# Attention steps with the values of two key steps in one run, another order for the maxima's scores, two merging DMAs a unit, and last units summed without GpSimd

## The chip, the cores and the metric

One core of a Trainium2 chip runs the whole kernel. The metric is the device time of one execution in microseconds. The median of three runs of the kernel before is 1054.57 us (1052.63 to 1055.07).

## The reference

A transformer block: attention with LoRA projections, residual and layer norm, then a mixture of experts (8 experts, one chosen per token, capacity 256) with a shared expert, residual and layer norm. The change touches attention alone:

```python
q = _split(lora_linear(x, Wq, bq, Bq, Aq))      # x: (2, 1024, 512), 16 heads of 32
k = _split(lora_linear(x, Wk, bk, Bk, Ak))
v = _split(lora_linear(x, Wv, bv, Bv, Av))
scores = jnp.einsum('bhqd,bhkd->bhqk', q, k) * SCALE
attn = jax.nn.softmax(scores, axis=-1)
out = jnp.einsum('bhqk,bhkd->bhqd', attn, v)
out = out.transpose(0, 2, 1, 3).reshape(B, L, H * hd)
return lora_linear(out, Wo, bo, Bo, Ao)
```

All of it is in float32. The kernel splits operands in a high and a low part[...] and adds the products.

## The kernel before, in words

Attention is cut into 16 units (NU): two batches, four groups of four heads, two halves of the queries (512 each). A unit has eight steps, one for each 128 keys; there are 128 steps (NS), numbered t, with u = t // 8 and k = t % 8. Step t does, for each of its four heads (the quarters q of the step):

- `st_step` (L611): the transposed scores `st`, 128 keys by 512 queries, one matmul on PE (TensorE) into a PSUM tile of the pool `one` (three tiles; L620), then the exponential on ACT into `pt` (L629). A `pt` tile holds two heads, 128 x 1024. There are 14 of them, so seven steps' worth.
- after each head, what the list `between[q]` holds.

What is put there:

- `s1_step` (L182): the scores a second time, not transposed, 12 steps ahead (LEAD), into a PSUM tile of `s1p` (three tiles; L189); VectorE (DVE) takes the maximum of each row (L197). One a quarter, so four a step and 32 a unit. `finish_max` transposes a unit's maxima on PE (`mp`, also a tile of `one`), and two DMAs put them beside the queries, so that `st` comes out with the maximum taken off. It is called with a quarter of the following unit's first step, number MPP.
- `av_step(t - 1)` (L633): the values of the step before: for each head a matmul with 32 output columns, four heads side by side in the array, summed over the eight steps in a PSUM tile `av{u}` (two such tiles). In a trace each of these float32 matmuls is two records, so a step has eight.
- `adds(t - 1)` (L648): the sums of the exponentials over keys. The table `ADDS` says, for a step of a unit, what is added: "b" names the tile that collects, "p" adds a tile to it on POOL (GpSimd), "v" on DVE, each for both tiles of a step (the two letters stand for the two tiles), and "d" is a DMA from POOL's queue that adds one step's tile into the next step's tile (a merging DMA; L656).
- `finish(u - 1)` (L666): matmuls with a matrix of ones sum the collected tile over its 128 rows into `sm` (a tile of `one`); the steps in `DIRECT` (step 7) go into it directly. For units below RDIR (13), ACT copies `sm` out and it goes by DRAM into a layout of 128 x 16, so that the reciprocal is short; from RDIR on DVE takes the reciprocal of 128 x 512 at once (L682).
- `invert(u - 1)` (L693): that short reciprocal, a store, and four DMAs that broadcast it back (`rb`). It stands after step 5.
- `normalize` (L706) in three parts: DVE multiplies `av` with the reciprocals (L711), ACT, or DVE for units in NRM_DVE, copies the high part (L716, L714), DVE subtracts to get the low part (L718).
- residual loads and adds (`load_res`, `add_res`, an add on POOL), and from step 65 on the output projection of the first batch (`oproj`), whose matmuls are spread over the steps.

Each engine works in the order in which the program lists its instructions; these steps are in a manual schedule (L763), so the order is the one written. SP, the queue of most DMAs, is such an engine too. A waiting instruction holds what stands behind it on its engine.

After the last step come `av_step`, `adds` and `finish` of unit 15, then output projections of the second batch and the first work of the experts, in an order that TAIL lists. The projections `op10` and o1 to o3 need unit 14 alone, o4 and later ones unit 15.

Of the kernel before, what the change touches and what calls it, by code (L numbers as in the profile page):

```python
# [20 lines left out]
NU = 16  # L21
# [11 lines left out]
LEAD = 12  # L33
LATE, OP_ONE = (0,), 1
NS = NU * 8
# [14 lines left out]
}  # L50
MAN3 = {mybir.EngineType.PE}
MAN4 = MAN2 - MAN3
DIRECT = (7,)
NO_DIR = (NU - 2,)
FIN, FINQ = 4, 1
REC = 5
NRM = 0
K_AT = 6
XTB = 5


ADDS = {
    None: {0: "bb0", 2: "dd1", 3: "pp3", 4: "pp4", 5: "pp2", 6: "pp5", 7: "pp6"},
    NU - 3: {0: "bb0", 2: "dd1", 3: "pp3", 4: "pp4", 5: "pp2", 7: "dd6 pp5"},
    NU - 2: {1: "bb1 dd0", 3: "dd2", 5: "dd4", 6: "vv3", 7: "vv6 vv7 vv5"},
    NU - 1: {0: "bb0", 1: "vp1", 2: "vp2", 3: "vp3", 4: "vp4", 5: "vp5", 6: "vv6"},
}
OPROJ_AT = (65, 67, 69, 71, 73, 75, 77, 79)
RES_AT = tuple(8 * i + (2 if i % 2 else 6) for i in range(8)) + (70, 74, 86, 90, 100, 102, 106, 110)
RES_ADDS = tuple(t + 3 for t in RES_AT[:14]) + (119, 120)  # L70
RB = 2
# [1 line left out]
AHEAD = 5  # L73
W2_END = {2: (0, 1, 2), 3: (3, 4), 4: (5,)}
W2_AT = {2: (0, 1), 3: (2, 3), 4: (4,), 5: (5,)}
MPJ, MPP = 0, 2
RDIR = NU - 3
FINE, NRME = 3, {NU - 2: 6, NU - 1: 5}
OPROJ1 = 0
NRM_DVE = (NU - 3, NU - 2)  # L80
ROOT_LAG, NORM_LAG = 1, 4
# [17 lines left out]
def kernel(  # L99
# [5 lines left out]
    def f(ap):  # L105
        return ap.bitcast(F32)
# [98 lines left out]
    def finish_max(u):  # L205
        mp = one.tile([P, 512], F32, name=f"mp{u}", tag="one")
        pe.transpose(mp[0:16, 0:P], mts[u], ident)
        mh = mp_.tile([16, P], F32R, name=f"mh{u}", tag="mh", bufs=2)
        ml = mp_.tile([16, P], F32R, name=f"ml{u}", tag="ml", bufs=2)
        act.copy(mh, mp[0:16, 0:P])  # L210
        dve.tensor_tensor(ml, mp[0:16, 0:P], f(mh), ALU.subtract)
        for i, m_ in enumerate((mh, ml)):
            sp.dma_start(
                out=f(Qs[u % 3][96 + i : 97 + i, :, :]).rearrange(
                    "o h (q t) -> o (h q) t", t=P
                ),
                in_=f(m_),
            )
# [382 lines left out]
    with ph2, tc.manual_schedule(engines={mybir.EngineType.PE}):  # L601
# [57 lines left out]
                        eng.tensor_tensor(accs[u, pr], accs[u, pr], pts[i, pr], ALU.add)  # L659

        def direct(u):
            return () if u in NO_DIR else DIRECT

        fin = {}

# [95 lines left out]
        op10 = oproj(1, 0, 3)  # L761
        steps = ExitStack()
        steps.enter_context(tc.manual_schedule(engines=MAN2))  # L763
        for t in range(NS):
            u, k = t // 8, t % 8
            if k == 0:
# [12 lines left out]
            if t in RES_AT:  # L779
                load_res(RES_AT.index(t))  # L780
            between = [[], [], [], []]
            if t + LEAD < NS:
                for q in range(4):
                    between[q].append(lambda q=q: s1_step(t + LEAD, q))
            elif t + LEAD == NS:
                between[0].append(lambda: finish_max(NU - 1))
            if t:
                between[1].append(lambda: av_step(t - 1))
                between[1].append(lambda: adds(t - 1))
                if u and k == (FINE if u == NU - 1 else FIN):  # L790
                    between[1 if u == NU - 1 else FINQ].append(lambda: finish(u - 1))
            if u:
                if k == NRM and 1 < u < NU - 1:
                    for q in range(3):
                        between[q].append(lambda q=q: normalize(u - 2, (q,)))
                if k == NRME.get(u):
                    for q in range(3):
                        between[(0, 3, 3)[q]].append(lambda q=q: normalize(u - 1, (q,)))
            if t in RES_ADDS:
                between[3].append(lambda: add_res(RES_ADDS.index(t)))  # L800
            st_step(t, between)
            if k == REC and 1 <= u <= RDIR:
                invert(u - 1)
            if t in OPROJ_AT:
                op0 = oproj(0, OPROJ_AT.index(t), OPER)
            if OPROJ_AT[0] <= t:
# [5 lines left out]
            later[:] = [(n - 1, fn) for n, fn in later if n]  # L812
            if t - NS >= OPROJ1:
                next(op10, None)
        av_step(NS - 1)
        adds(NS - 1)
        finish(NU - 1)
# [458 lines left out]
```

## Time and profile before

| | |
|---|---|
| median of three runs | 1054.57 us |
| the profiled execution | 1057.79 us |
| its span (first to last instruction) | 1056.1 us |
| mean granted TensorE clock | 0.992 |
| attention steps, first `st` of step 0 to that of step 127 | 155.82 to 601.15 us |
| first output projection after them | 614.54 us |
| first matmul of the shared expert | 640.82 us |

The page lists each engine's busy time, then groups of instructions by line: out<-in with shapes and count, then busy time, mean ns of one, and the idle time of that engine just before them with what ended most of it. PEld is TensorE's weight load, which runs beside matmuls. In a timeline a row has the start and the length in us, engine, line and tiles; rows of one kind in a row are merged with their count, and square brackets tell idle time before it and who ended it. Matmuls are pipelined, so a matmul's row of 0.40 us can be followed by the next after 0.235. A start to start distance is the cost; idle PE between two rows does not show where rows overlap.

Busy time by stretch (us from the span's start, busy us):

| stretch | PE | DVE | ACT | POOL |
|---|---|---|---|---|
| 225 to 255 | 29.47 | 23.49 | 20.29 | 29.47 |
| 285 to 315 | 30.00 | 24.40 | 19.86 | 29.77 |
| 375 to 405 | 29.75 | 20.82 | 14.73 | 26.60 |
| 525 to 555 | 30.00 | 24.32 | 19.85 | 30.00 |
| 585 to 605 (20 us) | 19.35 | 19.86 | 14.65 | 14.85 |
| 605 to 640 (35 us) | 28.72 | 26.58 | 9.48 | 19.45 |

The granted clock is 1.00 in all of these but the last, where it is 0.90.

### The profile page before, as it was taken

To read this page: it belongs to the slowest core of one execution; us is meant where nothing else is said; L and a number is where in the kernel's file an instruction comes from. 1 tells how busy PE (TensorE), PEld (TensorE's weight loads), DVE (VectorE), ACT (ScalarE), POOL (GpSimd) and SP (SyncE) were. 2 spreads that over 40 slices of the span, in tenths; PEclk is the share of its full clock that TensorE was granted. 3 is DMA by queue.
4 is the path that set the end of the run, shared out by engine and by line. 5 is a ranking of instruction groups with operands and counts; after the bars stand their busy time and mean duration, and the time that the engine had idled before them with its cause. 6 is when DMAs were issued, how large, how long until landed. Compare 5 with 4: busy or idle time off the path is not lost. (4 is left out here: it accounts for less than half of the span.)

```text
span 1056.1 us, 16556 instructions
## 1 busy us (share of the span) xinstructions
PE 1030.1 (98%) x5994; PEld 742.5 (70%) x5994; DVE 696.0 (66%) x1191; ACT 527.1 (50%) x1023; POOL 585.9 (55%) x407
## 2 busy tenths in 40 slices
PE   8999999999999999999999889999999999999995
PEld 6888774444444456544444359899999999999994
DVE  7732788778888877778887974233522557777752
ACT  5422216666666655566666716222222447555552
POOL 4000006999999986979995655000050046766674
PEclk9999999999999999999999989999999999999998
DMA  9866863454646553535648123000073456777721
GB/s 294 278 225 212 253 194 91 91 135 104 137 93 148 119 127 81 126 85 123 146 115 184 21 60 111 21 21 20 21 244 107 130 175 232 254 249 245 259 84 60
DMA packets 85449, 149.83 MB, mean 142 GB/s; under 512 B 15428, under 2 KB 24132, under 8 KB 85368
## 3 DMA queue, kind: packets, MB, share of 16 engines
q1 hardware_dynamic: 76344, 117.31, 37.5%
q0 software_dynamic: 9024, 31.48, 12.4%
q8 instruction: 47, 0.77, 0.3%
q14 instruction: 34, 0.28, 0.1%
HBM read 95.83 MB, written 33.78 MB: 123 GB/s over the span
## 5 line engine op out<-in xcount | busy, mean ns | idle before, releaser
L197 DVE TENSOR_REDUCE mt<-s 128x1 f32<-128x512 f32 x512 | 323.9, 681 | 79.7 <-PE s L189 79.3
L659 POOL TENSOR_TENSOR pt<-pt,pt 128x1024 f32<-128x1024 f32 x143 | 350.7, 2918 | 6.7 <-ACT pt L629 6.4
L629 ACT ACTIVATE pt<-st 128x512 f32<-128x512 f32 x512 | 269.1, 602 | 130.4 <-PE st L620 117.0
L620 PE MATMUL st<-qs,ks 98*128 98x512 f32 x512 | 213.2, 427 | 1.7 <-ACT pt L629 1.0
L189 PE MATMUL s<-ks,qs 96*128 96x512 f32 x512 | 200.3, 398 | 1.0 <-DVE mt L197 1.0
L620 PEld LDWEIGHTS st<-qs,ks 98*128 98x128 f32 x512 | 95.6, 189 | 133.5 <-issue 93.1
L656 POOL DMA_DIRECT2D pt<-pt x36 | 33.3, 1113 | 174.4 <-PE st L620 165.0
L890 PE MATMUL h<-xthe,w13s 128*128 128x256 f32 x704 | 130.0, 284 | 0.0
L878 POOL TENSOR_TENSOR w2s<-w2r,w2s 128x512 fp32r<-128x512 f32 x42 | 65.9, 1590 | 93.9 <-ACT w2s L877 93.6
L189 PEld LDWEIGHTS s<-ks,qs 96*128 96x128 f32 x512 | 97.1, 190 | 20.3 <-DVE mt L197 5.6
L890 PEld LDWEIGHTS h<-xthe,w13s 128*128 128x128 f32 x704 | 110.7, 191 | 0.3
L890 PE MATMUL h<-xtle,w13s 128*128 128x256 f32 x352 | 100.3, 285 | 0.0
L639 PE MATMUL av<-pt,vt 128*32 128x512 f32 x512 | 75.3, 605 | 0.0
L1038 POOL DMA_INDIRECT xd_d<-x1a,slot_i x8 | 7.9, 984 | 110.4 <-DVE slot_i L1035 108.3
L639 PE MATMUL av<-pt,x1b 128*32 128x512 f32 x512 | 68.2, 605 | 0.0
L890 PEld LDWEIGHTS h<-xtle,w13s 128*128 128x128 f32 x352 | 67.4, 191 | 0.7
L934 PE MATMUL y<-w2s,hs 128*128 128x512 f32 x260 | 60.9, 390 | 0.1
L934 PEld LDWEIGHTS y<-w2s,hs 128*128 128x128 f32 x260 | 48.2, 188 | 10.2 <-DVE hs L916 0.5
L331 ACT ACTIVATE oh<-o,bqk_sb 128x512 fp32r<-128x512 f32 x32 | 22.0, 690 | 57.8 <-PE o L316 53.0
L316 PE MATMUL o<-xh,wh 128*128 128x512 f32 x116 | 45.5, 392 | 0.3 <-DVE ol L332 0.3
L901 ACT ACTIVATE sl<-h 128x256 f32<-128x256 f32 x40 | 15.4, 385 | 60.5 <-PE h L890 59.2
L316 PE MATMUL o<-xh,wl 128*128 128x512 f32 x116 | 45.4, 391 | 0.0
(830 smaller groups left out, 1846.8 us busy)
## 6 DMA issues: line engine op xcount, KB each, us to landing
pt<-pt POOLq DMA_DIRECT2D x36, 512.0 KB, 6.4
x1a<-in_w_dram SPq DMA_DIRECT2D x24, 512.0 KB, 5.1
w2r<-in_w_dram SPq DMA_DIRECT2D x42, 256.0 KB, 3.4
qkd<-oh SPq DMA_DIRECT2D x32, 256.0 KB, 2.4
qkd<-ol SPq DMA_DIRECT2D x32, 256.0 KB, 2.4
x1b<-in_w_dram SPq DMA_DIRECT2D x16, 512.0 KB, 5.6
qs<-qkd SPq DMA_DIRECT2D x30, 256.0 KB, 4.5
ks<-qkd SPq DMA_DIRECT2D x18, 256.0 KB, 4.5
```

Source lines behind the costliest of these rows:

```text
L189: pe.matmul(s1, Qs[u % 3][0:96, h, qt * P : qt * P + P], Ks[g % 2][0:96, h, kh * 512 : kh * 512 + 512], start=True, stop=True,)
L197: dve.tensor_reduce(mts[u][:, c, kh : kh + 1], s1, AX.X, ALU.max)
L316: pe.matmul(o, lhs, rhs, start=k + i == 0, stop=k + i == KC + 1)
L331: act.activation(oh, o, AF.Identity, bias=bias)
L620: pe.matmul(sb, Ks[g % 2][:, h, kc * P : kc * P + P], Qs[u % 3][:, h, :], start=True, stop=True,)
L629: act.activation(pts[t, h // 2][:, h % 2, :], sb, AF.Exp, scale=SCALE)
L639: pe.matmul(avs[u][32 * h : 32 * h + 32, :], vts[g][:, kc, 32 * h : 32 * h + 32], pts[t, h // 2][:, h % 2, :], start=kc == 0, stop=kc == 7 ...
L656: pool.dma_start(out=pts[i + 1, pr], in_=pts[i, pr], accum_op=ALU.add)
L659: eng.tensor_tensor(accs[u, pr], accs[u, pr], pts[i, pr], ALU.add)
L878: pool.tensor_tensor(hl[:, 1, :], raw, f(hl[:, 0, :]), ALU.subtract)
L890: pe.matmul(hp[:, j * 256 : j * 256 + 256], lhs, rhs[:, k, :], start=n == 0, stop=n == 11,)
L934: pe.matmul(o, lhs, rhs, start=n == 0, stop=n == 16)
```

## The change

- Values: `av_step` is called at even t only, for steps t - 2 and t - 1 together, in quarter 3 (AVQ); the last two come after the loop.
- The maxima's scores are no longer one a quarter. The table S_AT gives for each of a unit's eight steps and each quarter how many stand before the values and how many after them. They are taken in the same order; the total of a unit stays 32.
- `adds` stands in quarter 3 too. In a normal unit two steps are merged by DMA (2 into 3, 6 into 7) where it was one (1 into 2), and POOL adds four steps (1, 4, 3, 5) where it added five. Steps 6 and 7 reach the sums through the direct step 7.
- Unit 13 is treated as a normal unit, its reciprocal by DRAM too (RDIR 14), with steps of its own for `invert` and `normalize`. Unit 14 has three merging DMAs and four steps added on DVE, now in steps 5 to 7 (as before, three DMAs; before, in steps 6 and 7). Unit 15 has two merging DMAs and three steps added on DVE, and steps 6 and 7 direct; before, POOL and DVE each added one of its two tiles for five steps, DVE both for step 6, and step 7 was direct.
- `finish`, `invert` and `normalize` get their place from tables: (units later, step, quarter). In a normal unit `finish` stays one unit later in step 4, quarter 1, `invert` moves from after step 5 to step 6, quarter 3, and the three parts of `normalize` move from step 0, quarters 0 to 2, to step 0 quarter 3, step 1 quarter 1 and step 1 quarter 3.
- The transpose of the maxima is called with the following unit's score number 1, not 2; the first batch's output projections start one step later.

```diff
-DIRECT = (7,)
-NO_DIR = (NU - 2,)
-FIN, FINQ = 4, 1
-REC = 5
-NRM = 0
+DIRECT = {None: (7,), NU - 2: (), NU - 1: (6, 7)}
+AVQ = 3
+FIN = {None: (1, 4, 1), NU - 3: (1, 3, 1), NU - 2: (1, 2, 3)}
+REC = {None: (1, 6, 3), NU - 3: (1, 6, 0)}
+NRM = {
+    None: ((2, 0, 3), (2, 1, 1), (2, 1, 3)),
+    NU - 3: ((2, 0, 2), (2, 0, 2), (2, 0, 2)),
+    NU - 2: ((1, 4, 1), (1, 4, 1), (1, 4, 1)),
+}
+S_AT = (
+    ((0, 0), (0, 1), (0, 1), (1, 0)), ((0, 1), (0, 1), (1, 1), (0, 0)),
+    ((0, 0), (2, 0), (1, 0), (0, 1)), ((0, 1), (0, 1), (0, 0), (1, 1)),
+    ((1, 0), (0, 1), (0, 2), (1, 1)), ((0, 1), (1, 0), (1, 0), (1, 0)),
+    ((0, 1), (0, 0), (1, 0), (1, 0)), ((0, 1), (0, 1), (0, 0), (1, 1)),
+)
 ADDS = {
-    None: {0: "bb0", 2: "dd1", 3: "pp3", 4: "pp4", 5: "pp2", 6: "pp5", 7: "pp6"},
-    NU - 3: {0: "bb0", 2: "dd1", 3: "pp3", 4: "pp4", 5: "pp2", 7: "dd6 pp5"},
-    NU - 2: {1: "bb1 dd0", 3: "dd2", 5: "dd4", 6: "vv3", 7: "vv6 vv7 vv5"},
-    NU - 1: {0: "bb0", 1: "vp1", 2: "vp2", 3: "vp3", 4: "vp4", 5: "vp5", 6: "vv6"},
+    None: {1: "bb0 pp1", 3: "dd2 pp4", 5: "pp3", 7: "dd6 pp5"},
+    NU - 2: {1: "bb1 dd0", 3: "dd2", 5: "dd4 vv6 vv3", 6: "vv7", 7: "vv5"},
+    NU - 1: {1: "bb1 dd0", 3: "dd2 vv4", 4: "vv5", 6: "vv3"},
 }
-OPROJ_AT = (65, 67, 69, 71, 73, 75, 77, 79)
+OPROJ_AT = (66, 68, 70, 72, 74, 76, 78, 80)
-MPJ, MPP = 0, 2
-RDIR = NU - 3
-FINE, NRME = 3, {NU - 2: 6, NU - 1: 5}
+MPJ, MPP = 0, 1
+RDIR = NU - 2
...
+        quarters = iter([(s_, q) for s_ in range(LEAD, NS) for q in range(4)])
+        def maxima():
+            for s_, q in quarters:
+                s1_step(s_, q)
+                return
+        def at_step(table, t, q):
+            for v in range(max(t // 8 - 2, 0), t // 8):
+                at = table.get(v, table[None])
+                at = at[q] if isinstance(at[0], tuple) else at
+                if (v + at[0]) * 8 + at[1] == t:
+                    yield v
...
-            if t + LEAD < NS:
-                for q in range(4):
-                    between[q].append(lambda q=q: s1_step(t + LEAD, q))
-            elif t + LEAD == NS:
-                between[0].append(lambda: finish_max(NU - 1))
+            for q in range(4):
+                between[q] += [maxima] * S_AT[k][q][0]
+            if t + LEAD == NS:
+                between[AVQ].append(lambda: finish_max(NU - 1))
+            if t and t % 2 == 0:
+                between[AVQ].append(lambda: (av_step(t - 2), av_step(t - 1)))
+            for v in at_step(FIN, t, 0):
+                between[FIN.get(v, FIN[None])[2]].append(lambda v=v: finish(v))
+            for q in range(4):
+                between[q] += [maxima] * S_AT[k][q][1]
             if t:
-                between[1].append(lambda: av_step(t - 1))
-                between[1].append(lambda: adds(t - 1))
-                if u and k == (FINE if u == NU - 1 else FIN):
-                    between[1 if u == NU - 1 else FINQ].append(lambda: finish(u - 1))
-            if u:
-                if k == NRM and 1 < u < NU - 1:
-                    for q in range(3):
-                        between[q].append(lambda q=q: normalize(u - 2, (q,)))
-                if k == NRME.get(u):
-                    for q in range(3):
-                        between[(0, 3, 3)[q]].append(lambda q=q: normalize(u - 1, (q,)))
+                between[AVQ].append(lambda: adds(t - 1))
+            for q in range(3):
+                for v in at_step(NRM, t, q):
+                    between[NRM.get(v, NRM[None])[q][2]].append(lambda v=v, q=q: normalize(v, (q,)))
+            for v in at_step(REC, t, 0):
+                if v < RDIR:
+                    between[REC.get(v, REC[None])[2]].append(lambda v=v: invert(v))
...
             st_step(t, between)
-            if k == REC and 1 <= u <= RDIR:
-                invert(u - 1)
...
+        av_step(NS - 2)
         av_step(NS - 1)
```

More of the change, by code (lines that the diff above doesn't have):

```diff
@@ L661, in direct @@
         def direct(u):
-            return () if u in NO_DIR else DIRECT
+            return DIRECT.get(u, DIRECT[None])
         fin = {}
```

## The prediction, made before the changed kernel ran

> **What bounds the kernel now.** I read the page first, to see which engine is full.
>
> ```profile
> PE 1030.1 (98%) x5994; PEld 742.5 (70%) x5994; DVE 696.0 (66%) x1191; ACT 527.1 (50%) x1023; POOL 585.9 (55%) x407
> L197 DVE TENSOR_REDUCE mt<-s 128x1 f32<-128x512 f32 x512 | 323.9, 681 | 79.7 <-PE s L189 79.3
> L659 POOL TENSOR_TENSOR pt<-pt,pt 128x1024 f32<-128x1024 f32 x143 | 350.7, 2918 | 6.7 <-ACT pt L629 6.4
> L629 ACT ACTIVATE pt<-st 128x512 f32<-128x512 f32 x512 | 269.1, 602 | 130.4 <-PE st L620 117.0
> ```
>
> PE is full, and in the attention steps ACT and DVE wait for PE, not PE for them. POOL is as full there: in a stretch of six units (209.1 to 370.1 us) it is busy 159.0 of 161.0 us, DVE 129.5, ACT 106.5. Next, the PE timeline of one step of that stretch.
>
> ```profile
> 257.86 1.06 PE L639 MATMUL av<-pt,x1b 128*32 128x512 f32 x8
> 258.85 0.50 PE L620 MATMUL st<-qs,ks 98*128 98x512 f32 x1
> 259.19 0.39 PE L189 MATMUL s<-ks,qs 96*128 96x512 f32 x1
> 259.43 0.39 PE L620 MATMUL st<-qs,ks 98*128 98x512 f32 x1
> ...
> 260.60 0.39 PE L189 MATMUL s<-ks,qs 96*128 96x512 f32 x1
> 260.92 1.07 PE L639 MATMUL av<-pt,x1b 128*32 128x512 f32 x8
> ```
>
> Scores follow each other every 0.235 us (259.19 to 259.43). The first after a run of values takes 0.34 until the next, and the run begins 0.32 after the last score. From av to av is 3.06 us. Eight scores at 0.235 are 1.88. The eight av records are two rounds of four, and the sums' matmuls of the same shape show 0.43 us a round (weight loads at 303.42, 303.84, 304.27), so 0.85. The remaining 0.33 us is what entering and leaving the 32-column shape costs. A unit is 26.6 us (first scores of units 3 to 8 start at 236.32, 262.96, 289.60, 316.27, 343.00, 369.63): 8 x 3.06, plus 1.71 for the four rounds of sums (joined to a value run), 0.24 for the transpose of maxima, 0.3 for a wait behind the copy of the sums.
>
> Last, the timeline at the end of attention, which is where PE does stop.
>
> ```profile
> 601.15 0.73 PE L620 MATMUL st<-qs,ks 98*128 98x512 f32 x2
> 602.40 1.21 DVE L659 TENSOR_TENSOR pt<-pt,pt 128x1024 f32<-128x1024 f32 x1
> 604.85 7.78 DVE L659 TENSOR_TENSOR pt<-pt,pt 128x1024 f32<-128x1024 f32 x3
> 609.40 1.40 PE L672 MATMUL sm<-pt,ones 128*32 128x512 f32 x4 [4.67 <-DVE pt L659]
> 612.68 1.92 PE L672 MATMUL sm<-pt,ones 128*32 128x512 f32 x4 [1.88 <-DVE pt L659]
> 614.54 0.80 PE L744 MATMUL op<-wo_h,at_h 128*128 128x512 f32 x1
> ```
>
> From the last step's first score (601.15) to the first output projection (614.54) 13.4 us pass, most of it waiting for unit 15's sum. After 614.54 PE has no stop over 0.6 us, so what is gained before it should last.
>
> **Part 1: values in pairs.** The change has one run of 16 records for two steps. Seen alone a unit saves four entries; but the sums now stand by themselves (two scores after a step's start, not behind a run), which adds one. Net 3 x 0.33 = 1.0 us, giving 25.6.
>
> What it costs: a pair's run lasts 1.95 us, in which ACT and DVE get nothing, and the same 16 scores come in the denser stretches between. Each kind has three PSUM tiles. A tile turns round in 0.40 (matmul) + 0.10 (to ACT's start) + 0.60 + 0.05 + 0.10 (weight load) = 1.25 us on ACT, and 0.40 + 0.04 + 0.68 + 0.05 + 0.10 = 1.27 on DVE; queued, ACT takes one every 0.48 us (four in 2.07) and DVE one every 0.60 (four in 2.48). I walked one unit of the new PE order with these numbers: each score starts at the later of the previous start + 0.235 and the release of the third tile before it. On the old order the walk gives 26.7 us (trace 26.6). On the new one it gives 26.4: 25.45 of matmuls, and 0.95 of new waits. The largest, 0.48, is in the third step (st twice in a row while ACT has the at_h copy of `normalize` in its queue); nine others of 0.01 to 0.11 stand where the table puts two st or two s together. So 0.3 us a unit, not 1.0. Changing each latency of the walk by 0.03 to 0.1 moves this gain between 0 and 0.7, which are my bounds. For units 2 to 7 and 11 to 13, 9 x 0.3 = 2.7. Units 0 and 1 gain 1.2 and 0.6 in the walk (the first values come two steps later, so four runs start as two). In units 8 to 10 the output projections' matmuls thin out the scores; between 0 and 1.0 each, I take 0.7: 2.0. Together 6.5 us until step 112.
>
> **Part 2: two merging DMAs a unit, four sums on POOL.** POOL's adds start every 2.34 us (294.43, 296.79 and 304.68, 307.01), a pair of DMA issues takes 1.15 of POOL, a residual add 1.05. Before: 10 x 2.34 + 1.15 + 1.05 = 25.6 of 26.6. After: 8 x 2.34 + 2 x 1.15 + 1.05 = 22.1 of 26.4. Since PE never waited for POOL in these units, this buys room and no time: 0. What it must not lose: the second DMA adds step 6 into step 7, is issued after the values run at the unit's end, and lands 4.5 and 7.0 us later (4.5 and 6.4 from each issue, 301.19 and 301.77). The ACT tile that reuses its source is needed 6.3 and about 11 us after that run, the sums 8.4 us after. The cover is 1.4 us at the narrowest; without it every microsecond costs 14 units a microsecond, in PE. Load contention decides that, so I keep 0 to 1 us a unit and take 0.
>
> **Part 3: moved steps.** `invert` stands after step 6's values instead of after step 5's scores. Its wait on DVE for the sums' rows (3.7 us after the copy) gets longer cover. The broadcast back takes about 5.0 us (reciprocal's end 230.26, last wait of the multiply's queue gone near 235), and the multiply follows 5.4 us later instead of 6.5. Queued behind it on DVE are the maxima, and behind those PE. Cover 0.4, plus some 0.8 us in which DVE has nothing at that place: 0, bounded by 1 us a unit. On SP its store and four broadcasts now stand just before the next unit's key and query loads; these start up to 2 us later, with four steps to go: 0. The projections one step later are the same matmuls: 0. Unit 13 goes by DRAM: DVE loses one 3.35 us reciprocal and gains one of 0.24; PE did not wait for it.
>
> **Part 4: the last two units.** In steps 116 to 127 the old order takes 2.65 us a step, each run waiting 0.35 for ACT's last exponentials. In pairs the values are two steps old, no wait; the walk gives 4.48 a pair. From step 112 to the last step's first score it comes to 41.8 us, where the trace has 48.0. Against that stands DVE. Unit 14's eight adds (1.21 each, as 602.40 shows) and unit 13's three `normalize` steps (2.07) are 11.8 us from step 118's exponentials on, so unit 14's sum is complete about 0.8 us after PE asks for it. Here a rule of the Trainium skill speaks against the change: by "SBUF — State Buffer", section "SBUF: two separate sides", a DVE operation with two SBUF inputs and a reading GpSimd operation lock each other out for a whole instruction. Two residual adds stand on POOL at steps 119 and 120. By the row nearest (DVE add at 575.64, 1.22 us; the POOL add that met it 1.94 instead of 1.33) POOL pays; by the rule DVE may wait 1.3 us for each, 2.7 in all. I take a wait of 1.5 us, bounds 0.8 to 3.5: 43.3, a gain of 4.7.
>
> Then unit 15: reciprocal 3.35, `normalize` 2.07 and six adds of 1.21 from unit 14's sums to its own, 12.7 us, with no POOL add beside them (with one they took 3.2 to 3.4 each, three in 7.78 above). That ends about 4 us after the last step's first score. PE meanwhile has four scores, the last pair's run and two direct groups of sums (0.85 each; one more than before), and reaches the add's group at 4.8. The projection starts at about 6.5 instead of 13.4: 6.9. The six projection matmuls that ran 0.43 apart after the long stop (614.70 to 616.83) come at 0.235: 1.2. If the adds slip behind POOL's split of the shared weights, which starts some 4 us after the last score, two of them cost 3.4: 4.5 us less.
>
> **Sum.** 6.5 + 0 + 0 + 4.7 + 6.9 + 1.2 = 19.3 us. The profiled execution took 1057.8 us (span 1056.1) and becomes 1038.5; the median of the runs stands 3.2 below that execution, 1054.6, and becomes 1035.
>
> **Rivals.** (A) The forecast, 1035: 0.5. (B) The short waits of the walk do not appear, since most are within 0.1 us: 0.7 more in nine units and a little more in the last ones, 8 us more, 1027: 0.2. For it: the old order shows hardly such waits. Against: its scores alternate strictly. (C) The waits are twice the walk's, or the adds slip: the loop loses what it gained, the end keeps 11, 1044: 0.2. For it: DVE would be at 84% with bursts, only three tiles deep. (D) Slower: the broadcast of reciprocals lands late. Loads of 128 to 512 KB run beside it now, and the multiply holds the maxima on DVE. It decides from about 2.7 us of lateness beyond the 5.4: minus the 1.2 of cover and slack, 1.5 us in 13 units undoes the 19. At 4 us late it is 13 x 2.8 = 36 less 19, 1072. Against it: the 52 broadcasts landed in 1.9 to 2.4 us each. 0.1. That the pairs are not formed is excluded: the changed program has 64 runs of eight value matmuls (two records each) where the old one has 128 runs of four, and POOL has 112 adds and 66 merging DMAs.
>
> **Range and chances.** A measurement tells about 0.2% (2 us) from no change. 1026 to 1050 covers A, B and C with the bounds above, and leaves D and a little of C out. Faster 0.87, same 0.03, slower 0.10.
>
> **What would show it.** In the profile after: av runs of x16 every second step; units 2 to 7 of 26.0 to 26.6 us; new idle time of PE in front of st and s ended by ACT pt and DVE mt, some 0.5 to 1 us a unit; POOL near 88% there; no wait of DVE av for a DMA; the gap from the last step's first score to the first op 6 to 8 us, the sums' wait for DVE under 3 us, DVE adds at 1.2. Wrong it is if units take over 27 us, if the multiply or a pt shows a wait for a DMA, or if the last adds still take 3 us each.

## The result, and the profile after it

The changed kernel takes 1096.2 us, median of 4 runs (1093.02 to 1098.86); the kernel before, on the same chip, 1054.82 (1052.63 to 1058.11). The ratio is 1.040, 95% interval 1.036 to 1.043: 41 us slower, where 1035 was forecast. The profiled execution took 1096.93 us (span 1095.2). Executions of the kernel before lie in two groups (on one chip 24 of 36 at 1051 to 1055 us and 12 at 1056 to 1059), and the profiled one, 1057.8, is of the upper, 3.2 us above the median.

First the page: the busy times by engine and the group of POOL's adds (busy time and mean ns; then the idle time before them and what ended it).

```profile
PE 1039.2 (95%) x6002; PEld 751.5 (69%) x6002; DVE 680.9 (62%) x1190; ACT 528.7 (48%) x1024; POOL 537.1 (49%) x406
...
L672 POOL TENSOR_TENSOR pt<-pt,pt 128x1024 f32<-128x1024 f32 x112 | 287.0, 2846 | 157.6 <-PE av L652 154.1
```

POOL has lost 49 us of work, as the prediction said, and none of it went to the others (ACT 1.6 us more, DVE 15 less), yet PE's share falls from 98 to 95%. So PE stops. The list of waits (us in total, times, longest) shows PE waiting for the maxima on VectorE, and two waits for a DMA; before, the multiply waited for none, and ScalarE 0.8 us for a merging one:

```profile
PEld s L202 <- DVE mt L210: 64.6, 112, 4.0
DVE av L724 <- DMA rb<-rd: 33.7, 12, 4.5
ACT pt L642 <- DMA pt<-pt: 21.7, 5, 5.5
```

Where PE stops is found by taking the first score of every step. Units 0 and 1 take 24.6 and 26.0 us, less than before. Units 2 to 7 take 29.3 to 32.1, where the walk said 26.4 and the kernel before took 26.6 to 27.5. Against undisturbed steps (taken as 1.99, 4.07, 1.89 and 6.67 us for key steps 1 to 4), units 2 to 7 and 11 to 13 lose 48.3 us in all: 21.2 in key step 1, 6.8 in step 2, 14.1 in step 3, 5.8 in step 4, 0.4 in step 0. (e3 below, without these DMAs, has 2.09 and 4.41 in steps 1 and 2 of the same units, so 4.0 of the 48.3 us are not theirs.) Units normalize in steps 0 and 1; the tile that needs the second merging DMA's source comes up in step 3.

The place to look at is the end of a unit, where the reciprocals go out. In the kernel before, the merging DMA and their store stand there so (first broadcast after the store: `rb`):

```profile
274.87 1.77 POOL L656 DMA_DIRECT2D pt<-pt  x2 [0.46 <-PE st L620]
...
284.69 0.34 SPq L697 DMA_DIRECT2D rd<-r  x1
...
286.11 1.73 SPq L700 DMA_DIRECT2D rb<-rd  x4
```

The DMA's two issues, 512 KB each, have landed by 281.86, 2.8 us ahead of the store. Now the end of unit 3 after the change, with the queues of SyncE (SPq) and GpSimd:

```profile
262.26 1.49 SPq L165 DMA_DIRECT2D ks<-qkd  x3
262.30 1.77 POOL L669 DMA_DIRECT2D pt<-pt  x2 [8.08 <-PE s L202]
...
267.30 0.34 SPq L710 DMA_DIRECT2D rd<-r  x1
...
273.17 2.08 SPq L713 DMA_DIRECT2D rb<-rd  x4
...
276.83 0.70 DVE L724 TENSOR_TENSOR av<-av,rb 128x512 f32<-128x512 f32 x1 [4.11 <-DMA rb<-rd]
```

The first merging DMA (2 into 3) goes out at 262.30, its second half at 262.88, landing at 272.98. The 8 KB store of the reciprocals goes out at 267.30, in the middle of it; the first broadcast, which waits for that store, leaves at 273.17: 5.9 us later, 0.2 us after the merging DMA. Before, the same step took 1.4 us (median). The trace also records every DMA packet, and they tell that the bytes themselves wait: the store's 128 packets of 64 bytes run 4.0 to 5.4 us after its issue (0.8 to 1.0 before), the last of them 0.02 us after the merging DMA's last packet of 4 KB. In ten of the eleven units where DMA and store leave 5.0 us apart this distance is 0.02 to 0.06 us. In units 8 and 9, where they leave 8.8 us apart, the store takes 1.5 and 1.9 us. The multiply runs 9.5 us after the store, where the prediction had 5.4, and VectorE stands 4.11 us before it with the maxima behind. PE's timeline in the same place:

```profile
271.48 1.92 PE L652 MATMUL av<-pt,x1b 128*32 128x512 f32 x16
...
274.63 0.39 PE L202 MATMUL s<-ks,qs 96*128 96x512 f32 x1
278.17 0.79 PE L202 MATMUL s<-ks,qs 96*128 96x512 f32 x1 [3.15 <-DVE mt L210]
278.76 1.48 PE L633 MATMUL st<-qs,ks 98*128 98x512 f32 x3
```

The pair's run is there as drawn (x16, 1.92 us). Then 3.5 us from one maxima score to the next, and after it the scores are slow. The windows (stretch, length, PE busy with its count, granted clock, DMA share, GB/s) show why:

```profile
266.00:274.00 8.00, 8.00 (x50) 1.00 0.76 167
...
278.10:284.00 5.90, 5.83 (x17) 0.50 1.04 223
284.00:290.00 6.00, 6.00 (x41) 1.00 0.61 152
```

After the stop the granted clock is 0.50 for some 6 us, then 1.00 again. The Trainium skill, "TensorE: Matmul & The Clock Gate", section "What's actually happening", has half rate after an idle window of about 3.4 us. The rate agrees; the clock fell sooner, at 277.2, 2.2 us after the last matmul's end. So lateness is paid more than once: multiply waits of 4.53, 4.11 and 4.29 us (units 2, 4 and 6) cost their units 5.2, 5.9 and 6.2 (4.8, 5.5 and 5.7 against the steps of e3). The loop up to key step 112 has eight such stretches, 3.4 or 6.8 us each and 40.8 together; the kernel before and e3 have none there. They cost at most half of that, 20 us (an estimate: half rate, and PE busy throughout).

In odd units the stop comes later. Timeline, key steps 0 and 3 of unit 5:

```profile
305.77 1.77 POOL L669 DMA_DIRECT2D pt<-pt  x2 [0.44 <-PE st L633]
...
314.59 3.05 ACT L642 ACTIVATE pt<-st 128x512 f32<-128x512 f32 x6 [2.60 <-DMA pt<-pt]
```

The second merging DMA (6 into 7) lands 8.7 and 11.0 us after its two issues, not 4.5 and 6.4 as the prediction had it, with the loads of Q beside it; ScalarE's exponentials wait for its source.

The end of attention, PE and VectorE:

```profile
649.56 1.20 PE L633 MATMUL st<-qs,ks 98*128 98x512 f32 x4
...
654.25 1.22 DVE L672 TENSOR_TENSOR pt<-pt,pt 128x1024 f32<-128x1024 f32 x1 [2.73 <-DMA pt<-pt]
655.53 1.05 PE L685 MATMUL sm<-pt,ones 128*32 128x512 f32 x4 [0.36 <-DVE pt L672]
...
656.51 0.51 PE L757 MATMUL op<-wo_h,at_h 128*128 128x512 f32 x1
```

VectorE's adds take 1.22 and the sums wait 0.36 for them. From the last step's third score (650.13; in the kernel before that is the 601.15 which the table ahead and the prediction give to the last step's first score) to the projection: 6.4 us, 6.5 forecast, 13.4 before.

So the loop up to key step 112 lost 46.6 us (397.3 to 443.9), from there to the last step's third score 2.3 (48.0 to 50.3), and after it the kernel gained 9.9 (7.0 up to the projection, 1.1 from there to the last matmul, 1.8 after that): 39 in all.

### The profile page after: what moved, and what is told of

Same layout as the page of the kernel before. It is cut to its first block, busy times and chain, and to the rows that moved or that the text cites. A ratio compares the mean times of both kernels' runs of the same rounds, so it can differ in the third digit from the quotient of the medians.

```text
span 1095.2 us, 16602 instructions
## 1 busy us (share of the span) xinstructions
PE 1039.2 (95%) x6002; PEld 751.5 (69%) x6002; DVE 680.9 (62%) x1190; ACT 528.7 (48%) x1024; POOL 537.1 (49%) x406
## 5 line engine op out<-in xcount | busy, mean ns | idle before, releaser
L210 DVE TENSOR_REDUCE mt<-s 128x1 f32<-128x512 f32 x512 | 319.7, 682 | 101.1 <-PE s L202 101.1
L672 POOL TENSOR_TENSOR pt<-pt,pt 128x1024 f32<-128x1024 f32 x112 | 287.0, 2846 | 157.6 <-PE av L652 154.1
L202 PE MATMUL s<-ks,qs 96*128 96x512 f32 x512 | 206.8, 430 | 23.2 <-DVE mt L210 23.1
L633 PE MATMUL st<-qs,ks 98*128 98x512 f32 x512 | 199.9, 426 | 15.1 <-ACT pt L642 13.3
L202 PEld LDWEIGHTS s<-ks,qs 96*128 96x128 f32 x512 | 99.7, 195 | 96.8 <-DVE mt L210 64.6
L633 PEld LDWEIGHTS st<-qs,ks 98*128 98x128 f32 x512 | 99.4, 196 | 81.2 <-ACT pt L642 39.3
L669 POOL DMA_DIRECT2D pt<-pt x66 | 59.1, 1043 | 120.7 <-PE s L202 73.1
L652 PE MATMUL av<-pt,vt 128*32 128x512 f32 x512 | 65.4, 625 | 5.1 <-DVE at_l L731 5.1
L652 PE MATMUL av<-pt,x1b 128*32 128x512 f32 x512 | 63.3, 613 | 0.0
L329 PE MATMUL o<-xl,wh 128*128 128x512 f32 x116 | 45.3, 391 | 0.0
```

Of the source, the lines that this page charges most:

```text
L202: pe.matmul(s1, Qs[u % 3][0:96, h, qt * P : qt * P + P], Ks[g % 2][0:96, h, kh * 512 : kh * 512 + 512], start=True, stop=True,)
L210: dve.tensor_reduce(mts[u][:, c, kh : kh + 1], s1, AX.X, ALU.max)
L329: pe.matmul(o, lhs, rhs, start=k + i == 0, stop=k + i == KC + 1)
L633: pe.matmul(sb, Ks[g % 2][:, h, kc * P : kc * P + P], Qs[u % 3][:, h, :], start=True, stop=True,)
L652: pe.matmul(avs[u][32 * h : 32 * h + 32, :], vts[g][:, kc, 32 * h : 32 * h + 32], pts[t, h // 2][:, h % 2, :], start=kc == 0, stop=kc == 7 ...
L669: pool.dma_start(out=pts[i + 1, pr], in_=pts[i, pr], accum_op=ALU.add)
```

## The experiments

The theories: (1) the first merging DMA holds the store of the reciprocals, the multiply is late, and it holds the maxima; (2) the second, late beside the loads, holds the exponentials; (3) the rival: pairs stall on three PSUM tiles a kind, whatever the DMAs do. All runs in one table. "Ratio" is to the kernel before on the same chip, with its interval; "loop" is from the first score to key step 112, "tail" from there to the last step's third score, "gap" from that to the projection, us of the profiled execution; "store" the median from the store of the reciprocals to the first broadcast over units 0 to 12; "multiply" its total wait for broadcasts. The first four ran on a chip where the kernel before took 1064.63 us: everything after the projection took some 10 us longer there (451 us, not 441), the attention steps were the same.

| run | ratio | loop | tail | gap | store | multiply |
|---|---|---|---|---|---|---|
| before | 1 | 397.3 | 48.0 | 13.4 | 1.43 | 0 |
| after | 1.040 (1.036-1.043) | 443.9 | 50.3 | 6.4 | 3.80 | 33.7 |
| e1 no first merging DMA | 1.0075 (1.0053-1.0096) | 408.1 | 49.6 | 6.4 | 1.42 | 1.3 |
| e2 no second | 1.036 (1.031-1.041) | 434.7 | 53.1 | 5.7 | 3.88 | 31.3 |
| e3 neither | 1.0043 (1.0024-1.0062) | 405.4 | 50.5 | 5.7 | 1.43 | 0.5 |
| e4 last unit's sums alone | 0.9943 (0.9927-0.9959) | 398.0 | 47.2 | 5.3 | 1.43 | 0 |
| e5 first one moved | 1.025 (1.021-1.028) | 427.2 | 50.5 | 6.4 | 1.42 | 1.2 |
| e6 moved, no second | 1.0063 (1.0043-1.0084) | 407.2 | 49.9 | 5.7 | 1.43 | 0.5 |
| e7 store by ScalarE | 1.038 (1.034-1.043) | 444.4 | 49.7 | 6.4 | 3.62 | 30.2 |
| e8 later normalization | 1.034 (1.029-1.039) | 440.7 | 53.3 | 6.4 | 3.88 | 7.9 |
| e9 merging DMAs alone | 1.012 (1.008-1.015) | 407.2 | 53.1 | 4.7 | 1.42 | 0 |
| e10 late loads | 1.0075 (1.0051-1.010) | 409.5 | 49.7 | 6.4 | 1.43 | 0 |
| e11 lighter unit 14 | 1.0043 (1.0031-1.0055) | 405.5 | 48.9 | 5.7 | 1.42 | 1.4 |
| e12 last two units | 0.9947 (0.9929-0.9964) | 397.8 | 48.0 | 5.3 | 1.42 | 0 |
| e13 e9 with late loads | 1.0105 (1.006-1.015) | 410.5 | 50.8 | 9.6 | 1.42 | 0 |
| e14 plain store | 1.009 (1.006-1.012) | 416.7 | 50.6 | 6.4 | 1.45 | 12.7 |

Tail and gap have to be read together: in e9, with unit 15's sums as before, the gap is 4.7 us, but PE has stopped in the tail before it (key step 3 of unit 15 takes 9.6 us for 4.4). The sum of the two is 61.4 us before, 56.7 after, 57.8 in e9, 52.5 in e4 and 53.3 in e12.

**e1: without the first merging DMA.**

```
-    None: {1: "bb0 pp1", 3: "dd2 pp4", 5: "pp3", 7: "dd6 pp5"},
+    None: {1: "bb0 pp1", 3: "pp2 pp4", 5: "pp3", 7: "dd6 pp5"},
```

> The kernel after, with the merging DMA of key step 2 into step 3 replaced by two GpSimd adds of step 2 into the accumulator (six adds more on GpSimd's side, none on TensorE's). Theory 1 (the store of the reciprocals queues behind that DMA, the broadcasts land late, the multiply blocks the maxima on VectorE): the stalls in key steps 1 and 2 go (28 of the 48 us of excess in nine units, about 35 to 40 us over all units with the stall at the head of the last unit), the waits of the multiply for the broadcasts fall from 33.7 us to under 10, time 1055 to 1065. Theory 2 (the other DMA, 6 into 7, lands late beside the loads of Q and K and holds ScalarE's exponentials): the multiply's waits may go, but the time stays at 1085 or more. Theory 3 (the pairs themselves stall through the three score tiles in PSUM, DMAs have nothing to do with it): 1096 within 5. In all three the waits of ScalarE for the merging DMA in key step 3 stay as they are (21.7 us).

The ratio falls by 3.2 points, the loop by 35.8 us. The timeline at the same place as above:

```profile
256.03 1.48 SPq L165 DMA_DIRECT2D ks<-qkd  x3
...
261.07 0.34 SPq L710 DMA_DIRECT2D rd<-r  x1
...
262.50 1.71 SPq L713 DMA_DIRECT2D rb<-rd  x4
...
266.40 0.69 DVE L724 TENSOR_TENSOR av<-av,rb 128x512 f32<-128x512 f32 x1
```

The loads of K leave as long before the store as they did, but now they are through when it comes: their last packet ends 0.1 us after its issue (2.8 us in the kernel after). The first broadcast follows 1.43 us after the store, the multiply waits for nothing here (1.3 us in all). Theory 1 holds, theory 3 falls. The forecast of 1055 to 1065 us means 1.000 to 1.010 of the kernel before on its chip; it came to 1.0075. Steps 3 and 4 still lose 13.4 us in nine units, and ScalarE still waits 19.0 us for the other merging DMA.

**e2 and e3: without the second, and with neither.**

```
-DIRECT = {None: (7,), NU - 2: (), NU - 1: (6, 7)}
+DIRECT = {None: (6, 7), NU - 2: (), NU - 1: (6, 7)}
...
-    None: {1: "bb0 pp1", 3: "dd2 pp4", 5: "pp3", 7: "dd6 pp5"},
+    None: {1: "bb0 pp1", 3: "dd2 pp4", 5: "pp3", 7: "pp5"},     (e2)
+    None: {1: "bb0 pp1", 3: "pp2 pp4", 5: "pp3", 7: "pp5"},     (e3)
```

> The kernel after, with the merging DMA of step 6 into step 7 left out; TensorE sums key step 6 directly instead (four more summing matmuls a unit, estimated at 0.85 us a unit, 11 us in all). Theory 2: the stalls in key steps 3 and 4 go (20 of the 48 us in nine units, about 25 over all), ScalarE's wait for a merging DMA (21.7 us) goes to near 0, the multiply's wait for the broadcasts (33.7 us) stays; net 1080 to 1086. Theory 1 alone: 1105. Theory 3: 1107.

> Both of the edits before together: no merging DMA in units 0 to 13. Theories 1 and 2 together: the units go back to the walk's 26.0 plus 0.85, the loop to the last unit takes 46 us less the 11 us of added sums, time 1045 to 1055, and no wait for a DMA is left on the multiply or on the exponentials. Theory 3: above 1090.

In e2 the stall of step 3 goes (14.1 to 0.8 us in nine units), those of steps 1 and 2 stay (26.7): the two losses are apart. The ratio, 1.036 and not the 1.024 to 1.030 expected, is a miss: the loop is 9 us shorter in spite of the added sums, but the tail is 2.8 longer. In e3 no stall is left: units of 27.2 us, of which the added sums are 0.80 (key step 4: 7.47 for 6.67). Without those, 26.4: the walk's number. The 1045 to 1055 us expected of e3 (0.991 to 1.000) had counted units of 26.0; it came to 1.0043. e1 against e3 gives the second merging DMA's price: 408.1 - (405.4 - 13 x 0.80) = 13.1 us.

**e4 and e12: the end alone, on the kernel before.**

```
+DIRECT = {NU - 1: (6, 7)}       (others (7,), unit 14 none; e12: unit 14 (7,) too)
...
-    NU - 1: {0: "bb0", 1: "vp1", 2: "vp2", 3: "vp3", 4: "vp4", 5: "vp5", 6: "vv6"},
+    NU - 1: {1: "bb1 dd0", 3: "dd2", 4: "vv4", 5: "vv5", 6: "vv3"},
-    NU - 2: {1: "bb1 dd0", 3: "dd2", 5: "dd4", 6: "vv3", 7: "vv6 vv7 vv5"},   (e12)
+    NU - 2: {1: "bb1 dd0", 3: "dd2", 5: "dd4", 6: "vv3", 7: "vv6 vv5"},       (e12)
```

> The kernel before, with only the last unit's sums changed: two merging DMAs, three adds on VectorE, steps 6 and 7 summed by TensorE, nothing on GpSimd. If the end of the change gained what the profiles say (46.6 us lost up to key step 112, 39.1 lost in all), it is worth about 8 to 11 us here: 1044 to 1047. If the gain at the end came from the pairs or from the table, under 4 us: 1051 or more.

> The kernel before with the change's sums of the last unit (as in the fourth experiment) and in unit 14 step 7 summed by TensorE in place of two adds on VectorE. No pairs, no merging DMA added before unit 15. Expected 0.5 to 1.5 us under the fourth experiment: ratio 0.992 to 0.995, units 0 to 13 as before at 26.65.

Both beat both kernels, by 0.57% and 0.53% against before; the intervals overlap, so neither is better. The gap falls from 13.4 to 5.3 us with no pair anywhere. The 8 to 11 us expected of e4 were about 6 by the ratio: the profiles show 8.9 less in tail and gap together, but against the kernel before in an execution 3.2 us above its median.

**e5 and e6: the first merging DMA at another place.**

```
-    None: {1: "bb0 pp1", 3: "dd2 pp4", 5: "pp3", 7: "dd6 pp5"},
+    None: {1: "bb1 dd0", 3: "pp2 pp3", 5: "pp4 pp5", 7: "dd6"},   (e5)
+    None: {1: "bb1 dd0", 3: "pp2 pp3", 5: "pp4 pp5"},             (e6; and direct 6, 7)
```

> The kernel after, with the same number of merging DMAs and of GpSimd adds, but the first merging DMA is of step 0 into step 1, issued at key step 2, and no longer of step 2 into 3 at key step 4 (the accumulator is step 1's tile, the adds are of steps 2 to 5). Theory 1 says it is the place and not the number: the store of the reciprocals at key step 6 finds no merging DMA in flight, takes 1.4 us to the first broadcast as in the first experiment, the multiply waits for nothing, and the stalls in key steps 1 and 2 go. The wait of the exponentials for the second merging DMA stays, 1 to 2 us a unit as in the first experiment: units of 26.5 to 28, ratio 0.995 to 1.005. Against it: if any second merging DMA in a unit overloads the queue, the multiply's waits stay above 20 us and the ratio at 1.02 or more.

> The experiment before, without the merging DMA of step 6 into 7 (TensorE sums both). No collision is left, four pairs of GpSimd adds as in the kernel after: units of 26.0 plus the 0.80 us of the four summing matmuls, 26.8, with key steps 1 and 2 back at 1.99 and 4.07 us if their 0.1 and 0.34 us without merging DMAs came from the fifth pair of adds; ratio 0.990 to 0.999.

In e5 the store is back at 1.42 and the multiply at 1.2 us: it is the place and not the number. But the ratio, 1.025, was not the 0.995 to 1.005 expected; key step 4 now loses 25.8 us in nine units, waiting for the sum. POOL's timeline:

```profile
238.96 11.77 POOL L672 TENSOR_TENSOR pt<-pt,pt 128x1024 f32<-128x1024 f32 x5
250.68 1.72 POOL L669 DMA_DIRECT2D pt<-pt  x2
...
253.05 2.39 POOL L669 DMA_DIRECT2D pt<-pt  x2
260.37 9.55 POOL L672 TENSOR_TENSOR pt<-pt,pt 128x1024 f32<-128x1024 f32 x4 [4.92 <-DMA pt<-pt]
```

The issue of 6 into 7 stands in POOL's queue behind the adds, so it leaves at 250.68 and the next unit's 0 into 1 only 2.4 us later; that one takes 7.2 and 9.1 us, and POOL waits 4.92 for it. In e6, alone, it lands in 4.4 to 4.5 and mostly 6.4 us and PE pays nothing: 27.2 us a unit as in e3, but for unit 12 (28.6). The forecast of 26.8 was wrong in taking e3's longer steps 1 and 2 for a cost of the fifth pair of adds. Step 2 is longer where a unit normalizes (4.41 us, in units 0 and 1, which do not, 4.07); step 1 takes 2.09 in unit 1 too. ScalarE's wait for a merging DMA is 27.0 us in e6 and costs nothing there: step 3 stays at 1.95 us. A wait counts by where PE stops, not by its size.

**e7: the store issued by ScalarE.**

```
-            sp.dma_start(out=rd.rearrange("h (j c) -> (h j) c", c=16), in_=r16)
+            act.dma_start(out=rd.rearrange("h (j c) -> (h j) c", c=16), in_=r16)
```

> The kernel after, with only the store of the reciprocals issued by ScalarE's queue and not by SyncE's. It parts two causes of the late store. If SyncE's own order holds it (the loads of K, issued before it on the same queue), the store takes 1.4 to 2 us again, the multiply's waits fall to under 10 us and the time by 25 us or more. If the merging DMA in flight holds it, whatever the queue, nothing changes: 1.035 to 1.045.

Nothing changes beyond the intervals: SyncE's order isn't what holds the store. The list of DMA issues shows the other queue (KB, median us to landing):

```profile
rd<-r ACTq DMA_DIRECT2D x14, 8.0 KB, 3.5
```

The list has 4.8 for the kernel after, but both are medians over the few landings that the traces tell (8 of 14 here, 6 there), not of the same units. Unit by unit the time from the store to the first broadcast stays within 0.6 us of that in the kernel after (units 0 to 12), and in ten of eleven the store's last packet follows the merging DMA's last one by 0.02 to 0.05 us, as there. This agrees with the Trainium skill, "DMA: Bandwidth & Descriptors", section "Issuing engines are not separate DMA queues": whatever engine starts them, all run on the same 16 DMA engines. Which of them took a packet no trace here tells.

**e8: the normalization about 2 us later.**

```
-    None: ((2, 0, 3), (2, 1, 1), (2, 1, 3)),
+    None: ((2, 1, 1), (2, 1, 3), (2, 2, 1)),
```

> The kernel after, with the three operations of the normalization about 2 us of the walk later (multiply in quarter 1 of key step 1, copy in its quarter 3, subtract in quarter 1 of key step 2), its DMAs as they are. Theory 1's second half (the harm comes from the multiply that stands in VectorE's queue ahead of the maxima): the multiply's waits fall from 33.7 to about 10 us (2 us less at each of 12), and the stalls of key steps 1 and 2 by as much less what the subtract now holds up ahead of the next weighted-value run: 8 to 20 us gained, ratio 1.020 to 1.032. If the normalization isn't what blocks, nothing is gained: 1.037 to 1.043.

The multiply's waits fall to 7.9 us as expected, the ratio by 0.6 point instead of 0.8 to 2.0, and the interval overlaps that of the kernel after. The list of waits tells where the rest went:

```profile
PEld av L652 <- DVE at_l L731: 24.2, 14, 5.3
...
DVE av L724 <- DMA rb<-rd: 7.9, 7, 1.5
```

The values run of the next unit but one needs the PSUM tile that the normalization frees (two such tiles). So the deadline has two faces, VectorE's queue and that tile, and the lateness must go, not the multiply.

**e9: the merging DMAs alone, on the kernel before.**

```
-    None: {0: "bb0", 2: "dd1", 3: "pp3", 4: "pp4", 5: "pp2", 6: "pp5", 7: "pp6"},
-    NU - 3: {0: "bb0", 2: "dd1", 3: "pp3", 4: "pp4", 5: "pp2", 7: "dd6 pp5"},
+    None: {0: "bb0", 1: "pp1", 3: "dd2", 4: "pp4", 5: "pp3", 6: "pp5", 7: "dd6"},
```

> The kernel before with only the change's sums in units 0 to 13 (step 2 merged into 3 at key step 4, step 6 into 7 at the head of the next unit, adds of 1, 3, 4, 5), without pairs and without the moved steps. Here the reciprocals' store goes out some 7 us after the first merging DMA and the multiply follows 6.5 us after the store, not 5.4. Theory 1 (it is the meeting of the two in time that costs): the store takes 2 to 4 us to the first broadcast, the multiply waits under 10 us in all. Theory 2: ScalarE's exponentials of key step 3 wait for the second merging DMA as after, 0.5 to 2 us a unit. Ratio 1.003 to 1.020. If two merging DMAs alone carry the whole loss, 1.03 or more; if they cost nothing without the pairs, 0.997 to 1.002.

The ratio is as expected; the store is not late at all, where 2 to 4 us were expected. Here 2 into 3 leaves 7.7 us ahead of the store (223.98, 231.70) and has landed 7.0 us after its first issue; the store takes 1.42, no broadcast is late. What is left, 9.9 us of loop, comes with the second one (from unit 2's head on 6.6 to 9.2 and 8.5 to 11.7 us) and sits mostly in step 4, where the sums stand (6.3 of 9.3 us in nine units); step 3, where theory 2 expected a wait, takes 3.06 us as before. The first collision needs the places that the change gave to this DMA and the store: there the distance is 5.0 us.

**e10 and e13: the loads' lines two key steps later** (e1 and e9, `if k == 0:` to `if k == 2:` ahead of the loads of K, Q and V).

> The first experiment's kernel (after without the first merging DMA) with the loads of Q, K and V at the unit's key step 2 in place of key step 0, so that the second merging DMA has a start of some 3 us on them. Theory 2 (the loads beside it make it late): it lands in 4.5 to 8 us and not 9 to 12, and ScalarE's waits for it fall from 19.0 us to under 6; the stalls in key step 3 (7.3 us in nine units) go. The loads themselves may now be late for the maxima of key step 4: a stall there, 0 to 3 us a unit, tells nothing against it. Time: 0.995 to 1.02 by the latter. If the second merging DMA is late whatever runs beside it, the waits stay at 15 us or more.

> The ninth experiment's kernel (before's walk with both merging DMAs) with the loads of Q, K and V at the unit's key step 2 in place of key step 0: here the second merging DMA is issued about 1 us into the unit and the loads 6 us into it, 5 us later. In the tenth experiment the head start was only 1.3 us, and the DMA took 6 to 7.5 us (first half) and 8 to 10 us (second half). If the loads beside it make it late, it now lands in 4.5 and 6.4 us in nearly every unit, as the other merging DMA does there. If it is late for another reason (the broadcasts of the reciprocals just before it, the place in the unit), it stays at 7 to 9 and 9 to 11.7 us as in the ninth. The time: the loads are nearer to their use, so between 1.000 and 1.02, no test.

Neither tests theory 2, for the edit moved the lines and not the loads: in SyncE's rows all but 6 of 222 leave within 0.6 us of where they left, counted from the unit's start (in e10 the loads of Q in unit 3 at 0.9, 1.3 and 1.8 us, as in e1). POOL issued the merging DMA 2.7 to 5.5 us into the unit, behind its adds: in odd units after all loads of Q, in most even ones after half of the loads or more. So it got no head start: in e10 it took mostly 5.6 to 8.4 and 7.7 to 10.0 us, ScalarE waited 14.9 us for it and step 3 lost 9.4 in nine units; in e13 it took 6.1 to 9.2 and 8.6 to 11.7, as in e9.

What speaks for the loads is the packet record of the kernel after. At the heads of units 1, 9, 10 and 14, where under 0.4 MB of other transfers run beside it, the second merging DMA has landed 6.9 to 7.6 us after its first issue; at the other ten, with 1.0 to 1.5 MB beside it, 9.2 to 12.9 us. Unit 14 has no load of Q, K or V at all, though the broadcasts run there too, and its halves land in 4.4 and 6.3 us (issues at 604.08 and 604.66). That is an observation, not an experiment. No run took the loads away.

**e11: fewer VectorE adds in unit 14** (e3, with steps 6 and 7 of unit 14 summed by TensorE).

```
-    NU - 2: {1: "bb1 dd0", 3: "dd2", 5: "dd4 vv6 vv3", 6: "vv7", 7: "vv5"},
+    NU - 2: {1: "bb1 dd0", 3: "dd2", 5: "dd4 vv3", 7: "vv5"},
```

> The third experiment's kernel (no merging DMA in units 0 to 13) with steps 6 and 7 of unit 14 summed by TensorE (eight more summing matmuls, 1.7 us) in place of four adds on VectorE. If those adds, standing ahead of unit 13's normalization on VectorE, are why unit 15's first run of weighted values waits (5 us in key step 2 of unit 15, 11.1 us in that step), then the wait falls to under 2 us and the stretch from key step 112 to the last step's third score falls from 50.5 to 45 to 48 us; ratio 0.9985 to 1.002. If the broadcasts or the merging DMAs hold it, 50 us or more, and 1.004 to 1.007.

In e3, with the broadcasts in time, the stop in unit 15 is there all the same:

```profile
584.75 9.98 DVE L672 TENSOR_TENSOR pt<-pt,pt 128x1024 f32<-128x1024 f32 x6 [3.14 <-ACT pt L642]
...
587.25 2.99 POOL L740 TENSOR_TENSOR x1b<-x1b,bo_bc 128x512 f32<-128x512 f32 x2
...
596.10 0.69 DVE L731 TENSOR_TENSOR at_l<-av,at_h 128x512 fp32r<-128x512 f32 x1
...
596.84 3.64 PE L652 MATMUL av<-pt,vt 128*32 128x512 f32 x16 [1.36 <-DVE at_l L731]
```

Six adds, one of them 4.30 us long beside POOL's two residual adds, stand ahead of unit 13's normalization, and unit 15's first run waits for that tile. e11 takes four adds out: that step falls from 11.1 to 9.6 us, the tail from 50.5 to 48.9, not to the 45 to 48 expected, and the ratio stays, as 1.7 us of sums come in. VectorE now waits there for unit 14's own merging DMAs (4.61 and 2.32 us) and 0.97 for the broadcasts. So the adds were a part of the stop, not the whole.

**e14: a plain store in the merging DMA's place** (e1, with step 2's tiles also copied to DRAM, which nothing reads).

```
+    None: {1: "bb0 pp1", 3: "pp2 cc2 pp4", 5: "pp3", 7: "dd6 pp5"},
...
+                        pool.dma_start(out=sc, in_=pts[i, pr])
```

> The first experiment's kernel (no first merging DMA) with, at the place of that DMA and on the same queue, a plain store of step 2's two tiles to DRAM: as many bytes, nothing added up, and nothing reads them. If any 512 KB transfer in flight holds the small store of the reciprocals, this store to first broadcast takes 3.3 to 5.9 us as after, the multiply waits for 25 to 35 us in all, ratio 1.03 to 1.04. If it is the accumulating kind that holds it (the loads of K in flight at the same place in the first experiment did not), 1.4 to 2.5 us, waits under 5 us, ratio 1.006 to 1.012.

Between the two. For the reciprocals of units 0, 2, 4, 6 and 10 the plain store is still in flight when theirs goes out, and it takes 3.5 to 4.5 us (after: 5.7 to 6.5); each time the first broadcast leaves 0.18 us after the plain store's landing, as it mostly leaves 0.2 us after the merging DMA's in the kernel after. So an accumulating DMA isn't needed to hold it. In the others it takes 1.41 to 1.77 (after: 3.3 to 3.9, units 7 and 8 aside), but there the plain store is no test: at 285.99 it goes out 6.4 us ahead of the reciprocals' store and has landed, in 3.0 and 4.6 us. With either kind, then, the store came out just behind the large transfer, and the accumulating one is longer in flight.

No run tells what the loads of K alone would do to it: in e1, unit 0's reciprocals aside, they are over when the store's packets run, 0.8 us after its issue.

## Why the prediction was wrong

- **Part 1, right in the plain units, wrong in the projections.** The walk's 26.4 us is what e3 shows (27.21 - 0.80), and its largest wait is there: the third step takes 4.41 us, 4.07 in units without a normalization. Nine units gained 3.0 us (2.7 forecast; 0.9 of it because unit 2 of the kernel before took 27.5 us), units 0 and 1 2.3 (1.8). Units 8 to 10 lost 3.1 where I took a gain of 2.0: e3 has 109.1 less 2.4 of sums against 103.6. That guess was not walked. In all 2.3 of 6.5.
- **Part 2, the step that failed.** "PE never waited for POOL in these units, this buys room and no time: 0." True of POOL. But only the second merging DMA was given a window; the first was costed as 1.15 us of POOL and nothing else, though it is a megabyte in flight for 7.0 us from its first issue. The collision could be seen in the rows of before: there the merging DMA leaves at 274.87, has landed by 281.9, and the store leaves at 284.69, 2.8 us clear. The change issues it after step 4's values, at the quarter where the pair's run ends, and the trace after has both 5.0 us apart: less than 7.0. The price could not be seen there. By these rows the store would be some 0.8 us late (an estimate: 2.0 of overlap and 0.2, less 1.4), within the 1.2 us of cover and slack. But the DMA itself took 8.1 to 8.6 us, and 10.5 to 11.1 where the loads of K ran beside it. Measured 35.8 us in all. The second one's bound, "0 to 1 us a unit and take 0", measured 13.1 us in 13 units: 1.0, at the end of the bound. (The starts that this part and the next give for POOL's rows and the reciprocal, 294.43, 301.19 or 230.26, are 0.31 us early against the trace; the distances are right.)
- **Part 3, right in its cover, wrong in what threatened it.** "Cover 0.4, plus some 0.8 us" was right as far as it went; in e1, e3 and e9 the multiply needs no more. The broadcast's 5.0 us was taken from a place where nothing large ran beside it.
- **Part 4, first half wrong.** From step 112 it forecast 43.3; it is 50.3, and 50.5 without merging DMAs. I timed unit 14's sum and not the PSUM tile of unit 13, which stands on VectorE behind unit 14's adds. Here the Trainium skill's rule ("SBUF — State Buffer", "SBUF: two separate sides") was nearer than my row: the add that met POOL's two took 3.28 us after and 4.30 in e3 for 1.21, 2.1 to 3.1 more, where I took 1.5 for the wait and the rule said 2.7. Which of the two goes first the starts do not tell: in e3 VectorE's add began 0.23 us ahead of POOL's.
- **Part 4, second half right.** 13.4 to 6.4 us (6.5 forecast, but from the first score, from which it is 15.5 to 7.0), and 1.1 for the projection matmuls (1.2 forecast); e4 shows that the shorter gap needs no other part of the change. The other 1.8 us lie after the last matmul (11.6 to 9.9 us). e6 has the same last units and takes 11.7 there, so they are not the end's gain; their cause is open.
- **The rivals.** D was the mechanism, given 0.1: reciprocals late, maxima held on VectorE, lateness of about 4 us (measured 1.9 to 5.0 at the store, waits of the multiply up to 4.5). Its sum of 36 us is what e1 measured, but partly by chance: the waits were fewer and each cost more, by the half clock after a stop. What it named as the cause, the loads, was half of it: without the merging DMA they are over in time (e1), but where they run beside it the store takes 5.7 to 6.5 us, without them 3.3 to 3.9. Against e3, steps 1 and 2 of the four units 2, 4, 6 and 12, which multiply with the later ones, lose 19.7 us, the other five of the nine 4.4. "52 broadcasts landed in 1.9 to 2.4" spoke of the broadcasts (the trace tells the landing of 11 of them); the store ahead of them was late.

The sum: 1038.5 was forecast for the profiled execution and 1096.9 measured, 58.4 apart. First merging DMA 35.8, second 13.1, pairs in the loop 4.2, tail 7.0, after the last matmul -1.8: 58.3.

## What to carry to other kernels

When an edit adds or moves a large DMA, draw its flight (issue to landing) on the time axis beside every small transfer on which an engine waits in order, and ask for clear air between them; here 2.8 us of clear air became an overlap of 2 by the quiet trace and of 3.1 to 6.2 as measured, for the flight grew too. A small DRAM round trip on a critical chain is priced by what is in flight at that moment, not by its median in a quiet trace. When a run is to move a transfer, read from its trace that it moved: e10 and e13 moved a program line and hardly a load. And try the parts of a change alone: the one part worth 0.6% stood beside pairs worth 0.2 to 0.3 us a unit and merging DMAs that cost 49 us.

## What the hardware showed beyond that

- An 8 KB store went from 1.4 to up to 6.5 us beside a merging DMA of two 512 KB transfers. Its packets ran only as the large transfer's last ones did, 0.02 to 0.06 us behind them in most units, from another engine's queue too (e7) and beside a plain store of that size (e14).
- The same merging DMA landed in 4.4 to 4.5 and mostly 6.3 to 6.5 us by itself, 7.2 and 9.1 right behind another one (e5), 8.7 to 10.5 and 11.0 to 12.3 at the heads of odd units, where loads run beside it.
- A stop of about 3.5 us was followed by some 6 us of half clock on TensorE. Multiply waits of 4.1 to 4.5 us cost their units 1.1 to 1.3 times as much (4.8 to 5.7 us).
